# One padding buffer, one queue: fetching the rows of a convolution band at another place, and moving the stores of the last but one chunk

## The chip, the cores and the metric

The kernel runs on one core of a Trainium2 chip. A core has five engines with queues of their own: TensorE (PE) multiplies matrices, VectorE (DVE) and ScalarE (ACT) work on tiles element by element, GpSimd (POOL) does small work and issues DMAs, and SyncE (SP) only issues DMAs. They meet through semaphores. The metric is the device time of one execution in microseconds (us); smaller is better. "PE" and "PEld" in the profile are TensorE's matmuls and its weight loads.

## What is computed

Two layers, each a residual around a group norm. The first is shifted-window attention, the second a depthwise 3x3 convolution with signs of weights. All data are float32.

```python
def reference(x, w_qkv, w_out, b_out, rel_pos_table, w):
    # x: (16, 56, 56, 384); 12 heads of 32; windows of 7 x 7, shifted by 3; 32 groups
    x = x + attention(_gn(x), w_qkv, w_out, b_out, rel_pos_table)
    x = x + depthwise(_gn(x), w)
    return x

# attention: roll by -3, q, k, v = x @ w_qkv.T; per window softmax(q k^T / sqrt(32) + rel + mask) v,
#            @ w_out.T + b_out, roll back
# depthwise: 3 x 3, SAME padding, kernel sign(w), one filter for each of the 384 channels
def _gn(v, G=32, eps=1e-5):
    g = v.reshape(B_, H_, W_, G, C_ // G)
    m = jnp.mean(g, axis=(1, 2, 4), keepdims=True)
    s = jnp.var(g, axis=(1, 2, 4), keepdims=True)
    return ((g - m) / jnp.sqrt(s + eps)).reshape(v.shape)
```

## The kernel before

**Tiling.** Channels lie on the 128 partitions, in NC = 3 blocks. An image has NS = 8 strips of 7 rows, a strip has 8 windows and is worked on in two units of 4 windows, so an image has NU = 16 units and the run 256. `all_units` walks over the units. For each, `heavy(u)` gives six lists of matmul work: queries and keys of the next strip (`query_key`, L472), its values (`value`, L485), the output projection (`project`, L656), and beside them the unit's own attention: `add_up` (L597, sums of the exponentials), `attend` (L617), `scores` (L526) of the next unit. `by_key` (L508) carries the values of a strip from `vq` to `v` by 16 DMAs on SP's queue, in two halves of eight, once each strip.

**PSUM.** Matmul outputs come from a pool of four banks (`bank`). The banks of the values are emptied by ScalarE, in the copy `vt` (L492).

**The convolution of the image before.** When an image's attention is done, its result lies in DRAM, in `mid` (written by GpSimd's queue, L680 and L682, strip by strip). The convolution of image b - 1 runs during the attention of image b. It goes over six chunks: two bands k of BR = 28 rows, times three channel blocks c. A chunk n = 3k + c takes these steps:

- `band` (L703): one DMA on SP's queue fetches 29 rows (of 59 columns) from `mid` into `xb`, a pool with a single buffer. It waits until the readers of the chunk before have left the buffer.
- `pad` (L748, ScalarE): normalizes the rows into a zero-bordered tile `hp` (two buffers). It reads `xb`.
- `middle` (L778, ScalarE): the residual and the centre tap into the sum `o` (two buffers). It is the last reader of `xb`.
- `tap` (L784, VectorE): eight taps, 128 x 1568 elements each.
- `turn_sum` (L791, VectorE) and `store` (L798, eight DMAs on SP's queue).

**What sets the order.** Each engine works through its queue in the order in which the program issues instructions, and that order is written out by hand. `at(when, f, ...)` enters a step at a time in units. Within a unit, after the i-th of the six lists, all entries are issued whose time is at most u + (i + 1) / 6. The names in `plan_conv` are `first`, the first unit of the image; `lead` = 3; and `step`, the units for one chunk: 2.6, and 1.95 for the last image but one. A chunk's taps start at `when` = first + 3 + step * n; its padding stands at when - 0.35 step, its middle at when - 0.25 step, its fetch at when - 0.75 step.

**The last image.** Nothing is left to hide its convolution behind. `plan_last` (its `at` times lie beyond the last unit, and the entries are issued in the order of these times) splits it: four chunks (k, c) with c < 2 go through VectorE's taps, and the third channel block, in four bands of LR = 14 rows, goes through TensorE as matmuls with diagonal matrices (`convolve`, L822 and L829, seven tiles of 2 rows each, in PSUM tiles of four and three), is copied out by ScalarE in `carry` (L837) and stored (L840). Chunks of k = 0 are turned by VectorE and stored by L798. Those of k = 1, the last two, go through `turn_late`: 14 transposes on TensorE (L855), copies to `xo` (L857), eight stores (L863) on SP's queue, for the very last chunk half of them on ScalarE's.

**After it** follow a small test whether the fast form of the softmax was safe (L1051 to L1063), which all engines read, and the program's end.

Of the kernel before, what the change touches and what calls it, by code (L numbers as in the profile page):

```python
# [34 lines left out]
def kernel(  # L35
# [55 lines left out]
    def bank(name):  # L91
        return ps.tile([P, 512], F32, tag="mm", name=name)
# [709 lines left out]

    summed = {}

    def convolve(b, k, c):

        hp, _ = padded[b, k, c]
        pitch = W + 2
        both = pitch + W
        hp, acc = (a.rearrange("p h w -> p (h w)") for a in (hp, outs[b, k, c]))  # L810
        tiles = LR * W // OT
        summed[k] = []
        for first in range(0, tiles, 4):
            n = min(4, tiles - first)
            pc = bank(f"pc_{k}_{first}")
            summed[k].append((first, n, pc))
            for i in range(n):
                here = pc[:both, i * P : (i + 1) * P]
                row = 2 * (first + i)
                for t in (0, 1, 2, 3, 5, 6, 7, 8):  # L820
                    dy, dx = divmod(t, 3)
                    nc.tensor.matmul(  # L822
                        here,
                        hp[:, (row + dy) * pitch + dx : (row + dy) * pitch + dx + both],
                        late_tiles["dg"][:, t],
                        start=(t == 0),
                        stop=False,
                    )
                nc.tensor.matmul(here, acc[:, row * pitch : row * pitch + both], ident, start=False, stop=True)  # L829
# [35 lines left out]
    def plan_last(b, first):  # L865

        chunks = [(k, c) for k in range(NB) for c in range(NC - 1)]
        bands_late = [(0, NC - 1), chunks[0], (1, NC - 1), chunks[1], (2, NC - 1), chunks[2], (3, NC - 1)]
        for n, (k, c) in enumerate(bands_late):
            at(first - 1.2 + 0.1 * n, band_late, b, k, c, 0)  # L870
            at(first - 0.04 + 0.001 * n, band_late, b, k, c, 1)
        at(first, norm_late, b)
        at(first + 0.1, center, b, nc.vector)
        for n, (k, c) in enumerate(chunks):
            when = first + 1 + n
            if n == len(chunks) - 1:
                for part in range(2):
                    at(when - 1.9, band_late, b, k, c, part)
            at(when - 0.6 if n else when - 0.13, pad, b, k, c)
            at(when - 0.5 if n else when - 0.12, middle, b, k, c, False, n == 0)  # L880
            for i, t in enumerate((0, 1, 2, 3, 5, 6, 7, 8)):
                at(when + i / 8, tap, b, k, c, t)
            if k == 0:
                at(when + 0.99, turn_sum, b, k, c)
                for part in range(2 * HPC):
                    at(when + 1.01 + 0.05 * part, store, b, k, c, part)
            else:
                for half in range(2):
                    at(when + 1.15 + 0.01 * half, turn_late, b, k, c, half, n == len(chunks) - 1)
            k, c = n, NC - 1  # L890
            at(when - 0.3 if n else when - 0.11, pad, b, k, c, True)
            at(when - 0.25 if n else when - 0.1, middle, b, k, c, True, n == 0)
            at(when + 0.1, convolve, b, k, c)
            at(when + 1.1, carry, b, k, c)


# [2 lines left out]
    def at(when, f, *args):  # L899
        side.setdefault(int(when), []).append((when, f, args))  # L900

    def plan_conv(p, first, step, lead, late, queue):

        at(first, norm_gather, (1, p), queue)
        at(first + 0.1, norm_scale, (1, p), queue)
        at(first + 0.2, center, p)
        first += lead
        for n in range(NB * NC):
            k, c = divmod(n, NC)
            when = first + step * n  # L910
            at(when - 0.75 * step, band, p, k, c)
            at(when - 0.35 * step, pad, p, k, c)
            at(when - 0.25 * step, middle, p, k, c)
            for i, t in enumerate((0, 1, 2, 3, 5, 6, 7, 8)):
                at(when + step * i / 9, tap, p, k, c, t)
            at(when + step * 8 / 9, turn_sum, p, k, c)
            for part in range(2 * HPC):
                at(when + step * 8 / 9 + late + 0.1 * part, store, p, k, c, part)
# [43 lines left out]
    def plan(last_queue):  # L962
        for b in range(1, B):
            plan_load(b)
            plan_conv(b - 1, NU * b, 2.6 if b < B - 1 else 1.95, 3, 0.4, nc.gpsimd)
        at(B * NU - 6, fetch_late)
        for t in range(9):
            at(B * NU - 5 + 0.3 * t, diagonal, t)
        plan_last(B - 1, B * NU)
# [156 lines left out]
```

## Time and profile before

| | |
|---|---|
| time, median of 3 runs | 4207.44 us (4202.64 to 4210.01) |
| the profiled execution's own time | 4213.37 us |
| its span, first to last instruction | 4211.4 us |
| mean granted TensorE clock | 0.988 |
| DMA: mean rate over the span | 104 GB/s |
| `band` (L703) | 90 DMAs of 855.5 KB |
| `v<-vq` (L508) | 2048 DMAs of 48 KB |
| stores of the sums (L798) | 736 DMAs of 98 KB |
| `tap` (L784) | 752 of 1833 ns |
| `pad` (L748), the 90 of the steady stretch | 1756 ns each |
| `middle` (L778) | 91 of 1705 ns |

A span is the time from the first to the last instruction of the core; the execution's own time lies 2 us above it. An engine's busy time is the time in which it runs instructions, and an idle stretch is put down to what ended it. A DMA line on "SPq" is the issue of the transfer, not the transfer. TensorE is busy nearly all of the time from the end of the start-up (about 85 us, the first unit) to about 4100 us.

### The profile page before, as it was taken

The numbers are of one execution on the slowest core, as the hardware profiler recorded it, in microseconds if no ns is written. First come the engines' busy times: TensorE is split into PE (matmuls) and PEld (weight loads), VectorE is DVE, ScalarE is ACT, GpSimd is POOL, SyncE is SP. The second block draws the span as 40 slices with busy tenths as digits, with TensorE's granted clock in tenths as the row PEclk, the third lists the DMA queues.
The fourth block names the chain that finished last, engine by engine and source line by source line (L and its number), as shares of the span: only waits on it lengthen the run. The fifth ranks groups of instructions, "written<-read, shape, count | busy, mean of one in ns | idle before, by whom it ended". The sixth has DMA issues, their size and how long they took to land.

```text
span 4211.4 us, 153120 instructions
## 1 busy us (share of the span) xinstructions
PE 4068.7 (97%) x67257; PEld 2565.1 (61%) x67257; DVE 3495.2 (83%) x3711; ACT 2232.3 (53%) x4654; POOL 1863.9 (44%) x3165
## 2 busy tenths in 40 slices
PE   5999999999999999999999999999999999999997
PEld 3666566565666666666566666666566566666656
DVE  3556889888898888889888888988989888888897
ACT  2545555555555555555555555655556555554552
POOL 5444435445453554445445453554445445451100
PEclk8999999999999999999999999999999999999998
DMA  4434555654565655556654565655555565554454
GB/s 92 79 63 85 97 107 116 112 111 92 111 122 93 124 109 101 99 106 117 112 115 97 103 121 93 124 112 99 98 112 112 109 121 96 102 119 83 96 109 107
DMA packets 1524021, 439.45 MB, mean 104 GB/s; under 512 B 1458970, under 2 KB 1473979, under 8 KB 1523346
## 3 DMA queue, kind: packets, MB, share of 16 engines
q1 hardware_dynamic: 1432680, 267.66, 37.3%
q0 software_dynamic: 87648, 159.12, 16.2%
q8 instruction: 532, 8.72, 0.9%
q10 hardware_dynamic: 3018, 2.78, 0.3%
q14 instruction: 143, 1.17, 0.1%
HBM read 169.63 MB, written 158.46 MB: 78 GB/s over the span
## 4 chain that ended last, share of the span: by engine, by line
PE 40%; issue 16%; DVE 14%; POOL 12%; DMA 10%; SPq 4%; ACT 3%; DVEq 0%; ACTq 0%; POOLq 0%
PE pq L472 16%; POOL xl L419 9%; PE pv L485 8%; PE py L656 8%; DVE o L784 6%; PE ps L526 3%; SPq L508 3%; PE po L617 3%; DMA xl<-in_x_dram 3%; DMA mid<-y 2%; PE ps L597 2%; DMA xb<-mid 2%; DVE e L543 1%; SPq L798 1%; DVE xt L436 1%
## 5 line engine op out<-in xcount | busy, mean ns | idle before, releaser
L472 PE MATMUL pq<-xn,wq_t 128*128 128x392 f32 x4608 | 1587.0, 497 | 0.3
L419 POOL DMA_DIRECT2D xl<-in_x_dram x1980 | 1332.8, 720 | 172.2 <-DMA mid<-y 59.6
L784 DVE SCALAR_TENSOR_TENSOR o<-hp,dw_t,o 128x1568 f32<-128x1568 f32 x752 | 1378.5, 1833 | 5.4
L472 PEld LDWEIGHTS pq<-xn,wq_t 128*128 128x128 f32 x4608 | 846.3, 188 | 596.6 <-issue 1.6
L485 PE MATMUL pv<-xn,wq_t 128*128 128x392 f32 x2304 | 827.3, 502 | 35.5 <-ACT vt L492 30.6
L656 PE MATMUL py<-ot,wo_t 128*128 128x392 f32 x2304 | 816.2, 499 | 15.1 <-DVE ot L645 15.1
L479 ACT COPY qk<-pq 128x392 f32<-128x392 f32 x768 | 369.2, 483 | 622.4 <-PE pq L472 621.2
L485 PEld LDWEIGHTS pv<-xn,wq_t 128*128 128x128 f32 x2304 | 425.9, 190 | 343.0 <-ACT vt L492 39.4
L676 POOL COPY y<-y 128x63 f32<-128x63 f32 x128 | 46.3, 362 | 1299.0 <-DVE y L664 1299.0
L656 PEld LDWEIGHTS py<-ot,wo_t 128*128 128x128 f32 x2304 | 426.3, 190 | 313.2 <-DVE ot L645 25.6
L637 DVE SCALAR_TENSOR_TENSOR ln<-ps,inv 128x588 f32<-128x588 f32 x256 | 195.3, 763 | 467.7 <-ACT inv L636 467.6
L561 ACT ACTIVATE e<-e 128x1176 f32<-128x1176 f32 x256 | 303.4, 1185 | 456.1 <-DVE e L543 454.2
L492 ACT COPY vt<-pv 128x392 f32<-128x392 f32 x384 | 188.9, 492 | 416.0 <-PE pv L485 415.4
L526 PEld LDWEIGHTS ps<-qk 32*64 32x64 f32 x24576 | 311.3, 132 | 156.5 <-issue 125.2
L617 PE MATMUL po<-e,v 49*32 49x49 f32 x24576 | 374.1, 212 | 12.3 <-DMA v<-vq 10.7
L617 PEld LDWEIGHTS po<-e,v 49*32 49x32 f32 x24576 | 362.6, 105 | 20.5 <-issue 10.2
L543 DVE SCALAR_TENSOR_TENSOR e<-ps,bias 128x1176 f32<-128x1176 f32 x256 | 347.7, 1358 | 17.2 <-PE ps L526 17.0
L526 PE MATMUL ps<-qk 32*64 32x49 f32 x24576 | 345.4, 226 | 9.0 <-issue 6.8
L448 ACT COPY x<-xt 128x196 f32<-128x196 f32 x720 | 225.8, 368 | 175.9 <-DVE xt L436 175.7
L496 DVE STREAM_TRANSPOSE vq<-vt 128x512 f32<-128x512 f32 x384 | 265.9, 694 | 9.6 <-ACT vt L492 6.5
L461 ACT ACTIVATE xn<-x,coef 128x392 f32<-128x392 f32 x384 | 247.1, 712 | 14.4 <-DMA coef<-cod 14.4
L664 DVE TENSOR_TENSOR y<-py,x 128x392 f32<-128x392 f32 x384 | 213.4, 556 | 44.7 <-PE py L656 44.1
(173 smaller groups left out, 3351.4 us busy)
## 6 DMA issues: line engine op xcount, KB each, us to landing
v<-vq SPq DMA_DIRECT2D x2048, 48.0 KB
xb<-mid SPq DMA_DIRECT2D x90, 855.5 KB
out_dram<-o SPq DMA_DIRECT2D x736, 98.0 KB
mid<-y POOLq DMA_DIRECT2D x112, 619.5 KB
xl<-in_x_dram POOLq DMA_DIRECT2D x1260, 52.5 KB
mid<-y POOLq DMA_DIRECT2D x15, 354.0 KB
xl<-in_x_dram POOLq DMA_DIRECT2D x180, 28.0 KB
mid<-y POOLq DMA_DIRECT2D x15, 265.5 KB
```

The costliest lines, as they stand in the source:

```text
L419: nc.gpsimd.dma_start(xz[i * D + lo : i * D + hi, c, k : k + n, :], flat[token : token + n * (hi - lo)].rearrange("(k t) c -> t k c", k=n) ...
L461: nc.scalar.activation(xn[:, c, :, :T], xs[s][:, c, :].rearrange("p (w t) -> p w t", t=T), AF.Identity, bias=coef[:, c, 1:2], scale=coef[: ...
L472: nc.tensor.matmul(pq[:, :ST].rearrange("p (w t) -> p w t", t=T), wq_t[:, c, m * P : (m + 1) * P], xn[:, c, :, :T], start=(c == 0), stop=( ...
L479: nc.scalar.copy(qk[:, m, :ST], pq[:, :ST])
L485: nc.tensor.matmul(pv[:, :ST].rearrange("p (w t) -> p w t", t=T), wq_t[:, c, 2 * C + m * P : 2 * C + (m + 1) * P], xn[:, c, :, :T], start= ...
L496: nc.vector.transpose(vq[:, :, :, m].rearrange("p h n d -> p n h d"), vt[:, m].rearrange("p (n w) (j b) -> p n (w j) b", w=2, b=D),)
L526: nc.tensor.matmul(pp[row * HT : (row + 1) * HT, i, k0 : k0 + T], qk[part, NC * fast + j, q0 : q0 + HT], qk[part, NC * (not fast) + j, q0 ...
L543: nc.vector.scalar_tensor_tensor(e, pp[:, :, : NC * 2 * T].rearrange("q i (n k) -> q i n k", k=T), QSCALE, bias[:, int(s % NS == NS - 1)]. ...
L561: nc.scalar.activation(flat, flat, AF.Exp, accum_out=reach[:, 0, u : u + 1])
L617: nc.tensor.matmul(po[w][i * D : (i + 1) * D, (2 * j + r) * T : (2 * j + r + 1) * T], vs[s][keys, n * 2 + r, h * D : (h + 1) * D], by_head ...
L656: nc.tensor.matmul(py[:, :ST], wo_t[:, c, m * P : (m + 1) * P], ots[s][:, c, :], start=(c == 0), stop=(c == NC - 1),)
L784: nc.vector.scalar_tensor_tensor(acc, by_half(hp[:, dy : dy + BR, dx : dx + W]), dw_t[:, c, t : t + 1], acc, ALU.mult, ALU.add)
```

## The change

There are two parts.

First, `band` is entered at when - 1.22 step in place of when - 0.75 step, but not earlier than half a unit into the image. The padding and the middle of the chunk before stand at when - 1.35 step and when - 1.25 step, so the fetch follows directly behind them in the program.

Second, in the last image's plan `convolve` is called once for each of its two PSUM tiles (`part` 0: four tiles, `part` 1: three), at when + 0.1 and when + 0.4, and `turn_late` moves from when + 1.15 to when + 1.3. Chunks lie one unit apart there, so the transposes of the last but one chunk come between the two parts of TensorE's last convolution, where they came behind both. For the last chunk they stay at the end.

```diff
-    def convolve(b, k, c):
+    def convolve(b, k, c, part):
...
-        summed[k] = []
-        for first in range(0, tiles, 4):
+        for first in (4 * part,):
             n = min(4, tiles - first)
             pc = bank(f"pc_{k}_{first}")
-            summed[k].append((first, n, pc))
+            summed.setdefault(k, []).append((first, n, pc))
...
                 for half in range(2):
-                    at(when + 1.15 + 0.01 * half, turn_late, b, k, c, half, n == len(chunks) - 1)
+                    at(when + 1.3 + 0.01 * half, turn_late, b, k, c, half, n == len(chunks) - 1)
...
-            at(when + 0.1, convolve, b, k, c)
+            at(when + 0.1, convolve, b, k, c, 0)
+            at(when + 0.4, convolve, b, k, c, 1)
             at(when + 1.1, carry, b, k, c)
...
             when = first + step * n
-            at(when - 0.75 * step, band, p, k, c)
+            at(max(when - 1.22 * step, first - lead + 0.5), band, p, k, c)
             at(when - 0.35 * step, pad, p, k, c)
             at(when - 0.25 * step, middle, p, k, c)
```

(`first` in the last block has had `lead` added, so `first - lead` is the image's first unit.)

## The prediction

> **What bounds the kernel now.** I read the page's busy shares first, then who waits for whom over the steady stretch from 400 to 4050 us, then the timeline around one such wait, then the windows with their clock, and last the chain of waits at the end.
>
> Page:
>
> ```profile
> PE 4068.7 (97%) x67257; PEld 2565.1 (61%) x67257; DVE 3495.2 (83%) x3711; ACT 2232.3 (53%) x4654; POOL 1863.9 (44%) x3165
> ```
>
> Waits of ScalarE and of TensorE, 400 to 4050 us (who waits, for what, total us, times, longest):
>
> ```profile
> ACT hp L748 <- DMA xb<-mid: 104.0, 16, 8.6
> ...
> PE pv L485 <- ACT vt L492: 30.6, 14, 2.7
> PE py L656 <- DVE ot L645: 12.1, 11, 2.0
> ```
>
> TensorE is the bound. Its largest repeated wait is 14 stalls of up to 2.7 us for ScalarE's copy of `vt`, and ScalarE stands still 16 times at `hp L748`, the padding, for a band that has not landed. The timeline of one image (start, length, engine, line, idle before in brackets) ties the two together:
>
> ```profile
> 1756.82 5.59 SPq L508 DMA_DIRECT2D v<-vq  x8
> ...
> 1762.55 0.74 PE L597 MATMUL ps<-e,ones 49*32 49x147 f32 x32
> 1762.59 0.48 SPq L703 DMA_DIRECT2D xb<-mid  x1
> ...
> 1767.78 1.75 ACT L748 ACTIVATE hp<-xb,coef 128x1624 f32<-128x1624 f32 x1 [7.59 <-DMA xb<-mid]
> 1769.44 0.47 ACT L492 COPY vt<-pv 128x392 f32<-128x392 f32 x1
> ...
> 1769.96 2.92 PE L485 MATMUL pv<-xn,wq_t 128*128 128x392 f32 x6 [2.67 <-ACT vt L492]
> ...
> 1771.40 0.77 DVE L637 SCALAR_TENSOR_TENSOR ln<-ps,inv 128x588 f32<-128x588 f32 x1 [6.86 <-ACT inv L636]
> ...
> 1782.81 0.73 PE L597 MATMUL ps<-e,ones 49*32 49x147 f32 x32
> ```
>
> The band (L703) leaves SP's queue at 1762.59, straight behind eight `v` transfers, although its buffer was free since 1727.49, when the L778 that reads the band before ended. It needs 5.2 us to the padding's start. ScalarE idles 7.59 us, the `vt` copy behind it is late, no PSUM bank comes free, TensorE stops, and VectorE idles 6.86 us.
>
> What one stall costs must be taken from unit to unit, not from the gap. A unit (half a strip, 256 in the run) begins with the L597 group; its starts in TensorE's timeline give 15.6 us for an even unit (1607.31 to 1622.91) and 15.2 for an odd one, but 20.26 from 1762.55 to 1782.81. Two window rows of the same length of work (us, PE, PEld, DVE, ACT, POOL busy, clock, DMA share, GB/s) show why:
>
> ```profile
> 1607.31:1622.91 15.60, 15.60 (x262) 9.83 (x261) 13.07 (x16) 6.15 (x13) 4.48 (x7) 1.00 0.38 77
> 1762.55:1782.81 20.26, 17.50 (x262) 10.50 (x261) 13.26 (x14) 11.10 (x24) 3.00 (x5) 0.92 0.35 93
> ```
>
> The same 262 matmuls take 2.76 us of idle time and 1.9 us more of busy time, at a clock of 0.92. Of the 14 stalled images, six have a clock record of 3.41 us at half speed behind the stall, and lose 3.9 to 5.1 us in this unit; the other eight lose 2.5 to 3.4 there and 1.2 to 2.8 in the next, where VectorE, held up 7 us, is late with L645 (the third wait line). I summed units 10, 11 and 12 of the image for all 14: 717.3 us, against 14 x (15.58 + 15.22 + 15.58) = 649.3. **The stall costs 68 us in the run**, 4.9 an image.
>
> **What the Trainium skill says.** "Perfetto Trace Analysis", Summary: the profiler window per engine type: for a DMA issued by a hardware queue the record ends before the data moves. The trace agrees: 0.48 us of issue, 5.2 us to the reader. "PSUM — Partial Sum Buffer", Engine vs sequencer instructions: the queues of ScalarE and VectorE are strictly first in, first out; that is why the `vt` copy stands behind a padding it has nothing to do with (7.59 us here). "TensorE: Matmul & The Clock Gate", Part 1, says the clock falls to half after an idle window of about 3.4 us and needs a busy one to recover; the 3.41 us records at 0.5 behind six stalls agree, so going without the stall also keeps the clock.
>
> **The change part by part.** The order of instructions on ScalarE, VectorE and GpSimd is the same in both kernels; only SP's queue (90 bands moved up) and TensorE's tail differ.
>
> Bands. A band moves from 0.75 to 1.22 chunk steps ahead, right behind the padding (1.35) and the middle (1.25) of the chunk before, which are the last readers of the one `xb` buffer. I laid the new order of SP on the times of this trace, and let each band start at the later of its place in the queue and the end of that L778:
> - Chunk 3, the stalled one: behind the `v` group that ends at 1728.22, free at 1727.49. It starts 34 us earlier, and its 5.2 us end 26 us ahead of 1760.2, where the padding could begin. The stall goes: -68.0.
> - Two further late bands (gaps of 1.21 and 0.88 at 1431.06 and 3447.85; their units took 16.32 and 16.23 where 15.22 is usual) go as well: -2.1.
> - Chunk 0: behind a store that ends at 1608.99; it must still wait for the last strip's `mid` writes, issued 1607.64 and 1608.29; the DMA packets of that queue are done by 1614. The next on SP is a `v` at 1620.13. Nothing lost.
> - Chunks 1 and 4: SP stands at the band until 1647.03 and 1773.57; next behind it are `v` groups released at 1652.46 and 1781.58. Cover 5.4 and 8.0 us (both sides move together once the stall is gone). Nothing lost.
> - Chunk 2: in front of stores at 1695.88, 0.5 us of issue. Stores have nobody close behind them (ScalarE's L778 waited 2.5 us in all for them in this stretch). Nothing lost.
> - Chunk 5: between the two halves of a `v` group (1814.07 and 1814.12). The packets of a band occupy the DMA engines for about 3.4 us, with the issue some 4. That `v` was issued by 1821.33, its matmuls begin at 1829.45: 8.1 us of cover, 4 left. Nothing lost; without cover it would be up to 4 us x 15.
>
> What stays at the place of the stall: the `v` of this strip is late by itself (its po group takes 2.04 us where 1.65 is usual), because four stores stand between its halves, and they stay; and the padding and the middle, 3.5 us of ScalarE, cost 0.37 us where chunk 0 pays them unstalled (unit 2: 15.95 against 15.58). I take 0.5 an image, bounds 0 and 0.8: +7.0 (0 to 11). VectorE is not late next: in the stalled unit it lost 6.86 us and the image only 3.7 to 5.9, so without the stall it is at least 1 us ahead of TensorE; over an image it is busy 218 of 252 us.
>
> Tail. From 4130 us the bound is VectorE's four times eight taps (L784, 15 us each). The transposes of the last but one chunk move from behind all seven tiles of TensorE's last convolution to behind the fourth, near 4185.5; their input was ready at 4179.6, so TensorE does not wait, and the last three tiles end near 4193.4, before the last tap ends at 4194.72. The final transposes do not move. What moves is SP's store queue:
>
> ```profile
> 4193.09 6.23 SPq L863 DMA_DIRECT2D out_dram<-xo  x8
> ...
> 4194.86 1.72 PE L855 MATMUL px<-ident,o 128*128 128x128 f32 x14 [1.14 <-DVE o L784]
> ...
> 4197.38 0.59 ACT L857 COPY xo<-px 128x512 f32<-128x512 f32 x1 [1.27 <-DVE xo L857]
> ...
> 4200.55 4.02 SPq L863 DMA_DIRECT2D out_dram<-xo  x4
> ```
>
> Eight stores leave about 6 us earlier, so the last four end not at 4204.58 but near 4199 (behind the copy ending 4197.97, 0.45 each). SP would be through its closing test 5 us earlier, but GpSimd's closing drain ends at 4208.63 and does not move, while SP's last ends at 4210.6. So -2.0; bounds 0 and -5.
>
> Sum: -68.0 - 2.1 + 7.0 - 2.0 = -65.1 us. The profiled execution took 4213.4 (span 4211.4), so 4148.3 for it; the median shown lies 5.9 lower, at 4207.44, which gives 4142.3. I add 2 us for small new collisions of the moved transfers (bounds 0 and 10): **4144**, 1.5% below.
>
> **The rivals.**
> A. *VectorE or `v` takes over in units 11 and 12.* For it: the waits on L645 and a VectorE busy 28.75 of 30.60 us in the units from 1669.40. Against it: those waits follow the stall alone. Then only unit 10's excess (49.6 of the 68.0) goes: -49.6 - 2.1 + 7.0 - 2.0 = -46.7, 4161; with the half clock kept for some other reason (six times 1.7 us) 4171.
> B. *Slower: SP's head stands in the way of `v`.* One place: chunk 5's band ahead of the second half of a `v` group. It decides only from 8.1 us of delay on; each us beyond costs one an image, 15 in the run, and the gain of 65 is eaten from 12.4 us of delay on. At 14 us: 15 x 5.9 = 88, so 4231. For it: the band's 855 KB go through the queue that `v` uses. Against it: the packets take 3.4 us.
> C. *No change:* the padding waits anyway, because the earlier band is itself held up at SP's head (by the L778 before it or by `mid`). 4207. Against it: the free time of 1727.49, 34 us ahead.
>
> **How the numbers follow.** Forecast 0.74, A 0.18, B 0.04, C 0.04. The forecast's own range is 4132 (the whole stall, the two bands and 5 us of the tail) to 4158 (4 us of the residue and 10 of collisions more). To leave out no more than 2 in 10 with A inside I take 4130 to 4174. A measurement of this kernel tells about 0.2% (8 us) from no change; forecast and A are faster by more, C is the same, B slower: 0.91, 0.04, 0.05.
>
> **What would show it.** Right: L748 no longer waits for `xb`, apart from the tail; no `pv` wait on `vt` above 1 us; no half clock between 102 and 4090 us; units of 15.6 and 15.2 us also at places 10 to 12; SP's last store before 4200 in terms of the old tail. Wrong: waits of po L617 for `v` that grow (B), of py L656 on L645 that stay (A), or an L703 that still leaves behind 1755 in the example (C). The forecast fails if the stalled units shrink less than the idle time they show.

## The result

| | before | changed |
|---|---|---|
| median of the runs | 4206.39 us (4 runs, 4202.64 to 4210.01) | 4131.12 us (4 runs, 4130.49 to 4134.16) |
| profiled execution, span | 4213.37, 4211.4 us | 4130.49, 4128.7 us |
| mean granted clock | 0.988 | 0.991 |

The ratio is 0.9822, with a 95% interval of 0.9809 to 0.9834: the changed kernel is 75 us faster. The two spans differ by 82.7 us, since the profiled execution of before lay 7 us above its median and that of the changed kernel lies at its own.

The waits of TensorE in the steady stretch of the changed kernel, 400 to 4000 us (who waits, for what, total us, times, longest), have one line left:

```profile
PE pv L485 <- DVE y L664: 3.5, 13, 0.4
```

The 14 waits for `vt` are gone, and those for L645 with them. The page of the changed kernel:

```profile
PE 4041.2 (98%) x67257; PEld 2554.0 (62%) x67257; DVE 3495.7 (85%) x3711; ACT 2237.9 (54%) x4654; POOL 1875.3 (45%) x3165
...
PE 68%; issue 10%; DVE 9%; POOL 7%; DMA 4%; ACT 1%; SPq 1%; DVEq 0%; ACTq 0%; POOLq 0%
```

The same work keeps TensorE busy for 27.5 us less (4068.7 before), so part of what was lost had lain in busy time. Six records of 3.41 us at half speed make some 10 us of it, the shorter groups of unit 14 (below) some 5 (both estimates from the traces); the rest was not taken apart. The second line is the chain of waits: 68% of it lies on TensorE, 40% before.

The same image and the same padding as in the prediction, in the timeline of the changed kernel:

```profile
1696.88 0.48 SPq L703 DMA_DIRECT2D xb<-mid  x1
...
1728.04 1.74 ACT L748 ACTIVATE hp<-xb,coef 128x1624 f32<-128x1624 f32 x1
...
1730.66 0.73 PE L597 MATMUL ps<-e,ones 49*32 49x147 f32 x32
1730.77 0.50 ACT L492 COPY vt<-pv 128x392 f32<-128x392 f32 x1 [1.00 <-PE pv L485]
1731.51 0.75 ACT L635 ACTIVATE ln<-ps,least 128x588 f32<-128x588 f32 x1 [0.24 <-PE ps L597]
1732.82 4.22 PE L485 MATMUL pv<-xn,wq_t 128*128 128x392 f32 x12
1733.11 0.77 DVE L637 SCALAR_TENSOR_TENSOR ln<-ps,inv 128x588 f32<-128x588 f32 x1 [0.64 <-ACT inv L636]
...
1746.31 0.74 PE L597 MATMUL ps<-e,ones 49*32 49x147 f32 x32
```

The band leaves 31 us ahead of the padding, the padding starts without a wait, and the `vt` copy now waits for the matmul and not the reverse. The window of this unit (us, then PE, PEld, DVE, ACT and POOL busy, clock, DMA share, GB/s):

```profile
1730.66:1746.31 15.65, 15.65 (x262) 9.88 (x261) 14.88 (x16) 9.95 (x23) 2.82 (x4) 1.00 0.46 122
```

It takes 15.65 us where it took 20.26, without an idle moment and at full clock. Between the start-up and 4017 us no half clock is recorded.

Where the 82.7 us come from, by the place of a unit in the image (times from the starts of the L597 groups in both traces; images 1 to 14 unless said):

```
units 10 to 12, the stall          64.7
unit 14                             6.1
units 0, 6 and 8                    4.8
unit 5, the two late bands          1.9
all other units                    -0.9
first image, last image             1.5 + 1.8
start-up; last unit to the end      0.4 + 2.4
```

The stall was expected. Unit 14 was not: a whole kind of gain that the prediction had at nothing. It is looked at in the second half of the experiments, and units 0, 6 and 8 in the comparison with the prediction.

### The profile page after: what moved, and what is told of

The parts are those of the page before. It is cut to its first block, busy times and chain, and to the rows that moved or that the text cites. A ratio compares the mean times of both kernels' runs of the same rounds, so it can differ in the third digit from the quotient of the medians.

```text
span 4128.7 us, 153178 instructions
## 1 busy us (share of the span) xinstructions
PE 4041.2 (98%) x67257; PEld 2554.0 (62%) x67257; DVE 3495.7 (85%) x3711; ACT 2237.9 (54%) x4654; POOL 1875.3 (45%) x3165
## 4 chain that ended last, share of the span: by engine, by line
PE 68%; issue 10%; DVE 9%; POOL 7%; DMA 4%; ACT 1%; SPq 1%; DVEq 0%; ACTq 0%; POOLq 0%
PE pq L472 28%; PE pv L485 14%; PE py L656 13%; PE ps L526 6%; PE po L617 5%; POOL xl L419 5%; DVE o L784 4%; PE ps L597 3%; DMA xl<-in_x_dram 1%; DMA mvd<-mv 1%; DVE e L543 1%; SPq L508 1%; POOL dev L268 1%; DVE st L452 1%; DVE y L664 1%
## 5 line engine op out<-in xcount | busy, mean ns | idle before, releaser
L485 PE MATMUL pv<-xn,wq_t 128*128 128x392 f32 x2304 | 814.5, 497 | 4.7 <-DVE y L664 3.5
L485 PEld LDWEIGHTS pv<-xn,wq_t 128*128 128x128 f32 x2304 | 423.6, 188 | 304.1 <-DVE y L664 5.3
L617 PE MATMUL po<-e,v 49*32 49x49 f32 x24576 | 368.9, 212 | 8.8 <-DMA v<-vq 7.9
L617 PEld LDWEIGHTS po<-e,v 49*32 49x32 f32 x24576 | 357.9, 105 | 16.4 <-issue 8.8
L664 DVE TENSOR_TENSOR y<-py,x 128x392 f32<-128x392 f32 x384 | 213.2, 555 | 51.2 <-PE py L656 47.9
```

The source lines that it names most:

```text
L485: nc.tensor.matmul(pv[:, :ST].rearrange("p (w t) -> p w t", t=T), wq_t[:, c, 2 * C + m * P : 2 * C + (m + 1) * P], xn[:, c, :, :T], start= ...
L617: nc.tensor.matmul(po[w][i * D : (i + 1) * D, (2 * j + r) * T : (2 * j + r + 1) * T], vs[s][keys, n * 2 + r, h * D : (h + 1) * D], by_head ...
L664: nc.vector.tensor_tensor(view.rearrange("p r (w c) -> p w r c", c=WIN), py[:, :ST].rearrange("p (w r c) -> p w r c", r=WIN, c=WIN), xs[s] ...
```

## The experiments: where the gain sits

Each is set against before, run on the same chip. `full` stands for the changed kernel.

**Bands alone.** The changed line of `plan_conv` in the kernel before, nothing else.

```diff
-            at(when - 0.75 * step, band, p, k, c)
+            at(max(when - 1.22 * step, first - lead + 0.5), band, p, k, c)
```

> The bands' new place without the change of the tail. If the 14 stalls (65 us by the unit times of the changed kernel) and the shorter groups of unit 14 (6 us) are the gain, this is 71 to 75 us faster than before and 2 to 3 us slower than the full change, with the steady units as there. If the stores of the last but one chunk are worth more than the 2.4 us that the two traces show, it falls short by more than 5 us.

Measured: 4135.26 us against 4210.76, ratio 0.9821 (0.9806 to 0.9836), 75.5 us faster. The bands are the gain.

**Tail alone.** The changed kernel with the old line in `plan_conv`.

> The change of the tail without the bands' new place. My theory: 2 us faster than before, at most 5, with all 14 stalls in place; from the last unit to the end 105.7 us in place of 108.1. Rival (the tail carries a fair part of the gain): 10 us or more.

Measured: 4208.75 us, ratio 0.9995 (0.9987 to 1.0004), 2.0 us faster; the interval reaches from 5 us faster to 2 slower. From the last unit to the end its trace takes 104.5 us in place of 108.1. Over all traces of this document that stretch takes 104.4 to 108.2 us (median 105.0) in the nine with the new tail and 108.1 to 110.4 (median 108.6) in the four with the old one, so a small gain is likely, though the medians of this run do not show it. The changed kernel shows what moved: its eight stores of the last but one chunk leave before the last transposes, the four last ones right behind the last copy (here lines are one lower than before):

```profile
4106.79 3.61 SPq L862 DMA_DIRECT2D out_dram<-xo  x8
...
4114.61 1.72 PE L854 MATMUL px<-ident,o 128*128 128x128 f32 x14 [1.64 <-DVE o L784]
...
4117.12 0.59 ACT L856 COPY xo<-px 128x512 f32<-128x512 f32 x1 [1.26 <-DVE xo L856]
...
4118.26 1.80 SPq L862 DMA_DIRECT2D out_dram<-xo  x4
```

Counted from the end of the last tap, SP's last store is through 4.3 us earlier than before (5.6 us against 9.9), but the program ends only 2.5 us earlier: SP now finishes 8.7 us before the end, where it had 6.9. That part of the gain is lost to the closing steps of the other engines, as the prediction had it.

**Chunk 3 alone.**

```diff
-            at(when - 0.75 * step, band, p, k, c)
+            at(when - (1.22 if n == 3 else 0.75) * step, band, p, k, c)
```

> Only chunk 3's band moves, the other five stay at 0.75 of a step, the tail is that of before. If the stall is the gain: 62 to 68 us faster than before; unit 14 keeps its 15.6 us. If the gain comes from spreading all bands (less contention of transfers), it is under 40 us.

Measured: 4151.37 us, ratio 0.986 (0.9845 to 0.9875), 59 us faster (53 to 65). By its trace units 10 to 12 gain 63.2 us and unit 14 gains 0.9. The median is a little below the expectation, its interval reaches into it. No other padding had cost much: with five bands at their old place ScalarE waits 1.5 us in all for `xb` from 400 to 4000 us.

**All but chunk 3.**

```diff
-            at(max(when - 1.22 * step, first - lead + 0.5), band, p, k, c)
+            at(when - 0.75 * step if n == 3 else max(when - 1.22 * step, first - lead + 0.5), band, p, k, c)
```

> All bands move but chunk 3's, and the tail as in the full change. If the stall is the gain, 10 to 14 us faster than before remain: unit 14 (6), two late bands and small ones (4), the tail (2.4); the 14 stalls stand in the trace. If spreading is the gain: 35 us or more.

Measured: 4191.55 us, ratio 0.9954 (0.9939 to 0.9969), 19 us faster, more than I expected. The stalls stand, here in its waits of TensorE from 400 to 4000 us:

```profile
PE pv L485 <- ACT vt L492: 30.8, 14, 3.3
PE py L656 <- DVE ot L645: 9.7, 9, 2.0
```

Its trace has 5.2 us of gain in unit 14, 3.7 in units 0, 6 and 8, 3.3 in the first and last image, 2.2 in unit 5, and 5.3 in units 10 to 12. Of these 5.3, 3.6 lie in unit 12, though the 14 stalls stand; chunk 3 alone gains as much there (3.5). So this part of the 68.0 us seems to need both the stall and another band at its old place, and the stall's own price, in units 10 and 11, is nearer to the 60.9 us that the changed kernel gains there. Together with chunk 3 alone (59 + 19 against 75 to 77 for everything) the parts add up.

**A band ahead of values that are due.** As full, but with chunk 3's band only a little further ahead than it was in the kernel before, in front of the second half of the values and not behind it.

```diff
-            at(max(when - 1.22 * step, first - lead + 0.5), band, p, k, c)
+            at(when - 0.85 * step if n == 3 else max(when - 1.22 * step, first - lead + 0.5), band, p, k, c)
```

> As the full change, but chunk 3's band stands at 0.85 of a step: in SP's queue between the two halves of a strip's values, where they have only 0.7 us to spare. If a band ahead of values that are due delays them by its own 3.4 to 4 us of transfer (rival B's mechanism), TensorE waits at the attention for the values and the band is still 1 to 2 us late for the padding: 2 to 4 us an image lost, 25 to 55 us slower than the full change, with waits of po for v. If the transfers share the DMA engines and nothing is pushed back, the values are not later and it is within 10 us of the full change.

Measured: 4182.72 us against 4208.23, ratio 0.9944 (0.9928 to 0.9961): 26 us faster than before, some 50 slower than full. Its timeline in the image of the example:

```profile
1743.47 0.39 SPq L703 DMA_DIRECT2D xb<-mid  x1
1743.91 3.56 SPq L798 DMA_DIRECT2D out_dram<-o  x3
1747.51 6.65 SPq L508 DMA_DIRECT2D v<-vq  x8
1750.37 1.74 ACT L748 ACTIVATE hp<-xb,coef 128x1624 f32<-128x1624 f32 x1
...
1754.22 0.28 PE L617 MATMUL po<-e,v 49*32 49x49 f32 x4 [0.54 <-DMA v<-vq]
...
1754.85 0.28 PE L617 MATMUL po<-e,v 49*32 49x49 f32 x4 [0.35 <-DMA v<-vq]
...
1756.18 0.98 PE L617 MATMUL po<-e,v 49*32 49x49 f32 x82 [0.62 <-DMA v<-vq]
```

The padding has its band and no longer waits at all (the expectation had it 1 to 2 us late), but the values are late, and TensorE stops at the attention piece by piece; in 14 images units 10 to 12 lose 54 us. So rival B's mechanism is real: in a place without cover a band in front of due values cost 54 us, four fifths of the 68 of the stall it cured. The changed kernel is fast because its place has cover, not because earlier is always better.

## The experiments: what unit 14 gained

In both traces I counted the semaphore waits that TensorE's queue executes in front of the attention group of a unit (L617), beside the time from the group's start to the next matmul's. Even units have them, odd ones have none (one group of full with seven is left out).

| waits | groups, before | median us | groups, full | median us |
|---|---|---|---|---|
| none | 127 | 1.20 | 127 | 1.21 |
| 5 | 0 | - | 16 | 1.20 |
| 6 | 14 | 1.32 | 13 | 1.32 |
| 8 | 114 | 1.59 | 98 | 1.59 |

The same group in TensorE's timeline, unit 14 of the example's image, first before, then full:

```profile
1829.45 1.64 PE L617 MATMUL po<-e,v 49*32 49x49 f32 x96
```

```profile
1793.36 1.27 PE L617 MATMUL po<-e,v 49*32 49x49 f32 x96
```

The traces carry the numbers of the semaphores. All DMAs of SP's queue take turns over eight of them (100 to 107), the 16 value transfers of a strip among them. The attention reads window 0 (first eight transfers) and window 1 (last eight) in turn, and waits for two transfers of the one, then for two of the other. In the example's unit 14 of before both windows need the same pairs of semaphores, 101 with 105 first, and so wait for each pair twice. With chunk 5's band between the halves, the second half's semaphores are shifted by one: window 1 begins with 102 and 106, the pair that window 0 needs next, and since its transfers are the later ones, window 0's wait is covered. Hence five waits and not eight, and 0.39 us less in 14 images.

If that is the reason, taking window 1 first should do the same everywhere, since its transfers are the later users of the same semaphores:

```diff
                 for i in range(HPC):
-                    for w in range(2):
+                    for w in (1, 0):
                         h = HPC * j + i
```

**On top of full:**

> The full change, and attend takes window 1 before window 0. Both windows' values come through the same eight semaphores, window 1's by later transfers, so a wait for window 1 makes that for window 0 needless: extra waits on TensorE's queue in the attention fall from 1203 to 714. In the traces a group with 8 such waits takes 1.59 us, with 6 1.32, with 5 or none 1.20. If the waits themselves cost this, 97 units lose 0.39 us each: 35 to 40 us faster than the full change. If the longer groups come from late values, nothing changes (within 5 us).

Measured: 4111.28 us against 4208.23, ratio 0.9768 (0.9755 to 0.9782); again on another chip 4110.29 against 4211.38, 0.9758. That is 20 to 25 us faster than full, half of what I expected. The waits in front of L617 as the trace of full shows them, and below as that of this kernel does (number, then shortest/median/longest in ns):

```profile
L617 PEldq EVENT_SEMAPHORE  x949: 51/51/51, 87.9 to 4012.4; - x190
```

```profile
L617 PEldq EVENT_SEMAPHORE  x557: 51/51/51, 93.6 to 3993.8; - x186
```

392 waits less, and the groups of units 0, 6, 8 and 12 fall to 1.20 us. Units 2 (about 2.0 us) and 10 (1.89) do not. In unit 2 the time to the next matmul holds a wait of that matmul itself: all 13 waits of L485 for VectorE's L664 lie there, in full (3.5 us together) as here (8.7), so what the group saved is lost again behind VectorE. In unit 10 it got worse (1.61 in full), since the first matmul now asks for the last half.

**On the kernel before:**

> The same reversal on the kernel before: 1250 extra waits become 681. If the waits cost what the groups show, 112 units save 0.39 us: about 40 us faster than before, with the 14 stalls still there. If the reversal only works together with the moved bands, less than 10 us.

Measured: 4183.68 us against 4208.23, ratio 0.9936 (0.9921 to 0.9952), 24.5 us faster, with the stalls in place. The reversal works without the moved bands, and again at some six tenths of the size expected: in its trace unit 2 gains nothing, and the stalled unit 10 takes 10 us more over 14 images.

**What is last in unit 10.** The prediction had named four stores between the halves of the values there. First they were put behind the values (chunk 1's stores 0.55 of a unit later), with window 1 first as above; full itself ran again beside it:

```diff
-                at(when + step * 8 / 9 + late + 0.1 * part, store, p, k, c, part)
+                at(when + step * 8 / 9 + late + (0.55 if n == 1 else 0.0) + 0.1 * part, store, p, k, c, part)
```

> The full change once more, on the chip of the next kernel, so that the two can be set against each other: 1.8% faster than before, units of 15.6 and 15.2 us.

> The full change with window 1 first, and chunk 1's eight stores entered 0.55 of a unit later, so that they stand behind the values of the next strip and not in front of and between their halves. If these stores make the values late at unit 10 (there the group takes 1.89 us with window 1 first, elsewhere 1.20), that unit falls to 15.2 us: 14 times 0.7, some 10 us faster than with window 1 first alone, 30 us faster than the full change. If the lateness comes from VectorE's turn of the values or from the transfer itself, nothing changes, and the later stores may hold up a sum's buffer.

Measured: full 4132.4 us (0.9815, 0.98 to 0.983), with the stores behind 4113.44 (0.9766, 0.9753 to 0.978): no faster than window 1 first alone. The group of unit 10 did fall from 1.89 to 1.20 us. But unit 11 rose to 15.87: the sum's buffer is freed late, ScalarE waits for it, and VectorE behind ScalarE. Its waits of ScalarE, 400 to 4000 us:

```profile
ACT o L778 <- DMA out_dram<-o: 43.0, 10, 5.9
```

Full has only 2.3 us of waits there. The last clause of the expectation was the right one: the stall had been moved, not removed.

Then all eight stores were put in front of the values instead, again with window 1 first:

```diff
-                at(when + step * 8 / 9 + late + 0.1 * part, store, p, k, c, part)
+                at(when + step * 8 / 9 + late + (0.02 if n == 1 else 0.1) * part, store, p, k, c, part)
```

> The full change with window 1 first once more, on the chip of the next kernel: 2.3% faster than before, unit 10 at 15.9 us.

> The full change with window 1 first, and chunk 1's eight stores entered 0.02 apart in place of 0.1, so that all eight stand in front of the next strip's values and none between their halves; the sum's buffer comes free earlier, not later. If the four stores between the halves make the values late, unit 10 falls from 15.9 to 15.2 us and unit 11 stays at 15.2: 8 to 10 us faster than with window 1 first alone. If the values only wait for VectorE, nothing changes.

Measured: 4099.02 us against 4110.29 for window 1 first alone, ratio to before 0.9731 (0.9718 to 0.9744). 11.3 us faster, a little more than expected, and the fastest of all: 112 us faster than before. In the example's image the group of unit 10, with window 1 first alone and then with the stores ahead, among what SP issues:

```profile
1716.09 2.63 SPq L798 DMA_DIRECT2D out_dram<-o  x4
1718.76 6.00 SPq L508 DMA_DIRECT2D v<-vq  x8
...
1726.20 1.42 PE L617 MATMUL po<-e,v 49*32 49x49 f32 x96
```

```profile
1704.60 9.89 SPq L508 DMA_DIRECT2D v<-vq  x13
1718.16 0.74 PE L597 MATMUL ps<-e,ones 49*32 49x147 f32 x32
1718.69 1.27 PE L617 MATMUL po<-e,v 49*32 49x49 f32 x96
```

The issue of the values ends 4.2 us ahead of their reader and not 1.4. TensorE's only wait left from 400 to 3960 us is

```profile
PE pv L485 <- DVE y L664: 9.5, 13, 0.9
```

## Why the prediction was right, point by point

- *The stall of chunk 3 goes, 68.0 us.* Right in mechanism and size: 64.7 by the traces, 59 (53 to 65) by the run that moves this band alone. The reading that carried it was the unit-to-unit time; the idle time on view (30.6 us of waits for `vt`) would have given half. That the clock would stay up was right too.
- *The residue, 7.0 us.* Too large: 3.3. Late values behind four stores exist; the last experiment showed them (11.3 us once the waits were out of the way). In the changed kernel they cost little: the group of unit 10 takes 1.67 us in images 1 to 14, those of units 0, 6, 8 and 12 take 1.56 to 1.58. The other part was misread: the 0.37 us of unit 2 was put down to the padding and the middle on ScalarE, but 0.28 of it is TensorE's wait for VectorE's L664, all of whose 13 cases lie in unit 2. What those two steps of ScalarE cost at the place of the stall was not taken apart.
- *Two late bands, 2.1.* Measured 1.9.
- *Chunks 0, 1, 2 and 4: nothing lost.* Right. No wait of L748 for `xb` is left in the steady stretch.
- *Chunk 5: nothing lost.* This term was wrong, on the good side: it is a gain of 6.1 us. I had asked what a band between the halves does to the transfers and not what it does to the semaphores.
- *Tail, -2.0.* Measured 2.4 in the traces and 2.0 in the run of the tail alone, whose interval includes nothing. SP's last store was to end before 4200 us in terms of the old tail; counted from the last tap it ended at 4200.3, a sign just missed.
- *2 us for new collisions.* None was found; the steady units other than those named differ by 0.9 us in all.
- *Units 0, 6 and 8.* Their 4.8 us were not foreseen; 4.1 of them are in unit 6, where before has irregular longer units (17.10 us in one image). A line of before's waits of TensorE, 400 to 4050 us, belongs to them and was passed over:

```profile
PE ps L526 <- issue: 6.8, 12, 1.2
```

Twelve times TensorE stops in `scores` for nothing that the profile names. Such stops stand in unit 6 in all four kernels that fetch chunk 2's band there (before, tail alone, chunk 3 alone, window 1 first on before), and in none of the nine that fetch it a unit earlier; the trace of full has none at all. Each of the twelve ends 1.3 to 2.2 us after the end of a 16 KB packet of the queue that the page lists as "q8 instruction" (one ends every 8 us or so), and in unit 6 the packet of that place ends up to 6.5 us into the unit in before, at most 4.8 in full. So the likely cause is that a band in flight (DMA share 1.00 from 1702 to 1706 us in the example's image) delays the fetch of TensorE's own instructions. No run was made to test it.

The forecast of 4144 us was 13 above the median of 4131: 6 from chunk 5's term, 4 from the residue, 2 from the collisions that did not come, 5 from units 0, 6 and 8 and 3 from the first and last image, less 7 or so because the profiled execution of before was slower than its median, so that a saving counted in its trace shows smaller in the medians. Rival A's waits left with the stall; B's mechanism exists but has cover in the changed kernel; C's wait did not come.

What stays open: how much of one stall is the half clock and how much the late bank was not taken apart, and why six of 14 stalls drop the clock and eight do not. An earlier L664 in unit 2, or a band split into smaller transfers there and elsewhere, was not tried.

## What to carry to other kernels

A fetch whose buffer is free early should stand in its queue where the buffer becomes free, ahead of unrelated transfers, but only where those transfers have cover: the same band a few places later in the queue, in front of values with 0.7 us to spare, gave two thirds of the gain back. Price a stall from the start of one repeated group to the next and not from the idle time shown, because part of the loss hides in busy time (here 30.6 us of waits for `vt` on view stood for some 65 lost). Where one engine waits for many transfers of a queue, ask first for those issued last, provided that they have landed by then: waits that are then covered disappear from the program. Where they had not (unit 10), the group grew instead, from 1.61 to 1.89 us.

## What the runs showed of the hardware that I had not expected

Semaphore waits in front of TensorE's short matmuls are not free. With up to five extra waits a group of 96 matmul records took 1.20 us, with six 1.32, with eight 1.59. The values were there: with the later window asked first, the groups with eight in units 0, 6, 8 and 12 fell to 1.20. Taking the waits out gave 20 to 25 us in each of two kernels. And a clock record of 3.41 us at half speed followed stalls whose wait on view was 1.3 to 2.7 us, in six of 14 cases; the other eight, of 2.0 to 2.6 us, had none. The prediction took these records as agreeing with an idle window of about 3.4 us, but no stall of before shows that much idle time. With the band in a place where values came late, the trace has ten records at half speed (47.8 us together, four of them of 6.83 us), with full none between the start-up and 4017 us.
